# Small VectorE results in SBUF, shifts on GpSimd, an ELU scaled by e, and rows by two transfers, in a four-layer graph stack

## The chip, the cores and the metric

The kernel runs on one core of one Trainium2 chip. The metric is the device time of one execution in microseconds; the time of a kernel is the median of its runs. The profile tells five engines apart: PE (TensorE, the matmuls, with its weight loads as PEld), DVE (VectorE), ACT (ScalarE), POOL (GpSimd) and SP (SyncE, which here only issues DMAs).

## The reference

The input `x` has 32 batches of 512 nodes with 128 features; `adj` is one 512 x 512 matrix of zeros and ones for all batches. Four graph layers follow one another, each as `x = layernorm(x + layer(x, adj))`. The norm is over the 128 features, with no gain:

```
layer 0:  e = x a_i + (x a_j)^T            # 512 x 512 per batch
          e = leaky((e - mean(e)) / sqrt(var(e) + 1e-14) * adj + adj)
          out = sigmoid(softmax(e, axis=1) x)
layer 1:  h = x Wp + bp; scores = leaky(h a_src + (h a_dst)^T), filled where adj <= 0
          g = relu(layernorm(softmax(scores) * adj @ h))
          z = relu(layernorm(((1 + eps) g + adj @ g) W1 + b1))
          out = relu(z W2 + b2 + g)
layer 2:  A = softmax over the edges (a 512 x 512 constant)
          out = diag(A) x W[0] + (A - diag(A)) x W[1] + bias
layer 3:  h = x W; scores as in layer 1 with self loops
          out = elu(softmax(scores) @ h)
```

## The kernel before

**Tiles.** A batch is a tile of 128 partitions by 4 blocks by 128 features, `[P, NB, D]`, so one node of four stands on each partition. Score matrices are four tiles of 128 x 512, transposed (`e_r`, `nm_g`, `e_a`), and the sixteen 128 x 128 products of a layer go into PSUM (`p_o_r`, `p_o_g`, `p_o_a`). The suffixes name the layers: `_r` is layer 0, `_g` layer 1, `_t` layer 2, `_a` layer 3.

**Order.** No loop of the source sets the order in which instructions stand. A `Recorder` takes down every operation with what it reads and writes; `ORDER`, a compressed string, then says which of the operations that are ready is issued next, over all 32 batches and all engines. Each engine works through its list strictly in that order. So the batches overlap: layer 0 of one batch stands beside layer 3 of another. The costs in `cost` only choose buffers in `order()` and the few `warm` transposes that fill early PE gaps. Since every instruction is emitted by the recorder's `emit`, nearly all of the profile has one line, L434, and groups are told apart by the names of their tiles.

**PSUM.** Seven banks of 128 x 512 go round in a ring (`bank`). The eighth bank is `own`: half of it holds the constant `a_ij`, and in the rest `corner` (L516) gives small results a fixed place, four turns of each. Into it DVE writes the per-node maxima `top` of layers 1 and 3 (by the accumulator output of `any_g`, `any_a`, a `tensor_tensor_reduce`), mean and variance `mv` of the norms of layers 0 and 3 (by `bn_aggr`), the product `mr`, and in the statistics of layer 0 `mean_r`, a second copy of `dev_r`, and `sq_r`. In the profile all of these are called `own`.

**Norms.** `normalised` (L881, layers 0 and 3) takes `bn_stats` and `bn_aggr` on DVE, adds epsilon on DVE (`ve`), takes the power -1/2 on POOL (`rs`), multiplies mean by it on DVE (`mr`), makes the shift on DVE (`sh`), and lets ACT write `x = rs * y + sh` in four pieces. `scale_of` (L869, layers 1 and 2, whose mean is zero) does the epsilon and the power on POOL.

**Rows.** A column `[128, 4]` is needed as a row on all partitions in three places. `rows_of` (L922) does this with four PE transposes of a broadcast column into a bank; the row of layer 0, `p_s_r`, is made so. `rows_by_dma` (L928) does it for `top`: DVE transposes in blocks of 32 (`turned`), four DMAs on SP's queue write 4 x 32 elements each to a line in HBM (`linem_g`, `linem_a`), and one DMA reads the line back to all partitions (`m_g`, `m_a`).

**The ELU of layer 3** (L1193 to L1204): `po` is the unnormalised product in two banks and `rz` the reciprocal of its sums. ACT takes `ex = exp(po * rz)` in four pieces; POOL takes `min(ex / e, 1)` over 128 x 512; DVE takes the maximum of `po * rz` and that, in four pieces, in place in PSUM, and adds `x` in two pieces to get `y_a`. (The product carries an added 1, for which the division by e makes up.)

Of the kernel before, what the change touches and what calls it, by code (L numbers as in the profile page):

```python
# [14 lines left out]
AF = mybir.ActivationFunctionType  # L15
ALU = mybir.AluOpType

P = 128
# [17 lines left out]
TURNS = 4  # L36
# [9 lines left out]
c-k#m2bSxqmIaBNqd>uSh5O$BJ%*nDyn1t2JC!Zj2u|2Rs%>L}X}Ytq)2(lxw7qZ_-`l3PZ6lBRFaN&(d;O80^Up7C|M?Za_1`i2ckSf+`S<I1|Gt~1h  # L46
2C5}Ilu1D=Xu}sxadFMU$||Qeto?@@1M`>^P(sHyk9@`{hH6~{Y##kyk6w}+^>7!{`J5A^M3z_e8|7wpYQwq-{0R4ebfK_{D(ex^Y!mnd%pjJy<g4#d0
s!Rez`yQSN*O(q{^S~pYKb5*_Zi!-+!Jd?%(^KU;nCqzutH$<oioy`Sq2r?;knm=llKr;Xm(7yxw20`)hu_p7aXuar_zMGk&)3&(EK9#cz6ie*XFWH-1
LIFZ%a8{Mz~T{>?wx<@cYFKm8wi_CI(3rR~q3_Ryd9-TGG}<5hp^ul+9JC;!h+%ReRm_d9=OEH3M>VtzvX3Lyvmqo=Q_`5EU-GkWKW56K4~#<#EG^OfR
f&gVSq*PPkJ_B`>r?x<hSEH6=H>EgQ;nLp)KzG8mzJC+phoZ`Fp{BG^1q_3RP@&3HN;{Edd9bcb_7ks#q|9oEIm3<t?yT%yuD5;f{;tK=R5Yjt_cYnVy  # L50
*%U&(^XoXn(R*w$l@ddlCDr^+IfnXq$NFFzv5vHch{th+m`gtLSz^Q_M!)jw^$P3frRTG^BgY)$m1AqY_3~-8#d_45%5j#GV{J8*FvCcp{I}$@og?10m
(cq0(;ob&ttpjpwt1Y#`8AJz<QpGqPqp=a;MtEp@x@us>#VhY>UBRyDWhBkUn}u$?P{&e*iec`d9K`g=p*-z8HbBrC&|x~?)(07bB@{TKKq3sN5`aXI`
Yx0zcKX05t6mto{zQ1HEp%_84osGw%KBj+n$HD=TG_hndpnxnE9F4J@09+;f~85@vz<5j_Ev@&#<Gta`UAWmr_N@v8(p0eL{V?)7gMHTYr0h`0}yu`F>
~I;`K$Ji`4UHe##%@HQwp^xvub>pEF+H*X6Dsb6xiOy)N^8`}q6&{5sR#=6D(ZpMOm^x4G(Lvgv<*zh2KB{#>`wS?ltT*CuOoXj7xsHJ}TdGr5>_{OCN
gHM-mWWAqnBt^fRSe}13vPboj<`T8{<{rO2rGJBz<a2sj7j$`=eGmiB+eEj<z?%6+|@h-08&ZK|1SN`RzSMI@<$GP<R`!1*RJmWduzx{i@UiUGdyFKAP
+<DhBE4s#=ua)>&W=2_HPl+m|fY|wSRo@XAzf%%P#xwFGs*ZSx5~>Qe*U?NUF56^NGC+kh#u3HSQ4M_su!-xsioq<JDKA++wtcP=6!PKi=^CQM5w^m$c
9vz~YegZL!YAjPWo9_D(pfHivP3e)@X_KU7lsS`Et%(rCK7B@Q6fOCiB>R3RV?p&<|J@R@|KuqiTdOy%f&~gu|P_g^_F<=H{whP8%0aUxTgTf-y(Kwg|
L`+RMCbi*+e3{l3NfV?9zv=h@6wof+#CQ;RT1$Lg`I%NvtI->_i3{L=-y}fpZE<;TRaez<c)F?npwCs3FxLJVGl@q)<{2ahxs6sAP5`9X8m|fg#p-lLX
>}vKv`6`Uo1Rq{)bBbkq_*Wj@ln^L_V@icD$3@(J0AQq)U{w}OzWH1nI?#lC5`%Z-t3V;hq)bFm||%<tQVeG>d9HpcKCb7z=7UO8J&%JHH$#Wx%j3l@C
CMgdY={3tid@u2ubkw;GXj!)QR@n^$Sl=svo&8ua?2u9UTC62OFv-wRCFA|r#**9{qHDN}Wl0<OsaG(&i$GctjgEz+NzV96iWME~C-gu#V-7zYbf?a-B  # L60
JAS$oEr}6SGlXboY~S&2H(Ksk_L@HDI1b^2OS!VN?|jV}--HBU1hq&dQF+&z@ZIjjV3kCOY_dvHqV$!NMtG^cmcm&QA`%fiL(Yubky)!Y@0g(|S}(LQh
#I9@MP$IHEo!yzR7b3XkS67h(TZuCkyfy5xY{`lPNS+eOhHwHP+?)aJ(SQ^XvCHaO1Pn@G^$WYSXx#@qpy_N9oIz%ESwYVHs_pYPFbyR93><Yi9DKJ?@
H}V8KO7B3PF}A@x)!kt_<)Kf9<C2W(d&@Iw%s7=pG2)&_pO=?Tp4KmQsT{A)ChZ^@hl6ilK?$spDw1g!nn@JhJR0+AbIsqetwV#5`EGn2(@QlE8NAEz)
KUp%SrKtE6f}Sz>jlJDRhNQKAW*Pu>UTBJS4vnBw9D{4SMHQpmnFuy+QCRJ{Q%!k$d*(+w9~GS=Bivk9Yx>(UiqRr~~&oxu(5WmqJeLIST7=^#Q}Ob%N
iENV<GRTmdfmY#Ty-0~buXxwMW6a*fnTFh9ilSrVv2bZ1G)+P)fk}Ek2D;(-3sNknLhdn^8zI&2=y?|oEvJUWwHiyizXGp=GDJsrXWAbLU>a(a`G>j7j
an+H^-4MRJW{C;RgxFZwIM!;|jC;l~J@4@jELuQW^09e~Ab?w;jBsoD&bddZ6)e5R8ZTP{w1~eUTEOS&ZttF4Djf^YSCTzT*@{IjUgs%~I%O~NRit`qx
laYHBE2fuAuHakWF1}<BTbaj)+(E;TB#t_G)f(KGXZBl=_6<zyrwEuMI@r%Ys?~~DtS;saf|GTsA@=7A^Lfy9yL@)^12$-uELsi`Y1K)s5RG8Ggz-S%s
kYDOhkv5=1?PPsWNDY1l|pQby09Nx^}l~)~j7tydsLCU*W#b>$t9!d6ZJZhzSS22I}TI-E{7Dqd}yd$n8jZbPza>a=J00QqHu#n9d~`TM0ds0<CzZHB!
1zXW?F|Z^nYx@7%UVY9*DR?J}`XAV$B4x%KTauqF_Za~z#KZjwt>YDPitvZgXvuV=caz7Y~SM?t+jC(%D?l_(VB2vx_hx)xz>46LG2PHEF<>jd$VSL;L
%bRrh42$<5*;D<UEebgiM0-5`y0g*9kx?b1y6Timi%uh_YLm|)hT0}Cp#8YC)@9wY_?Q>c0AXYrY(6lApU;SJ$k7%%&eQ~Wu4`t_%;(bGyAb-#g{vLi<  # L70
+op|Ie^<XWV2i`nc-9Cy_p2{M@IAzU>~)B;$EEw(o+p1jr$q+m{XFM$y<VxjpiA!v9X|T&BKJ+=xbk_FaCzwZ(QwowlG9cH)9$-8R2J^BGzT$W78Zo28
<H351AScQl2hZk?(5Wty^e}LG<9ZV{(wr3m~;$a@#_1LAgkS|?$G$zfTV@c2OQDOS4zoIH%Eco-3-WrY)m^K)*%H^XIPd#fM;Qgo?e5ZB2*&>B;_RNuq
=_DilpTc#~3`Fz<-%ynka2d3r&^vbUIjVINF^<Xz6^SM2pE;htr`8@j$I|ms_ZlLr-JQ5P0bTw7F`RGON7vh$is>n#vb8@Lo7?^DLUT#A8EyT8Hv>60j
bmQ_|o_UcwLAq7#}HEes<kWDVRyLnRaZ(Nu@DNhn8-N+URMjRxz<@KT2*+*7wZC(M3BpaIo@Oz}YfqFOWY3%E!tfIss}Sz$rNLLY+ZinST=31N*mC+;-
&wP5~v33#3HM*_*ZSV*5LAj9zd*E~RZl>}*35wN1K*^;j43sXaLXpfHl2Gnkqv1&S?c8Bsz4hO7_8=iQHrXxBDkFhe%gAry5ld3S*dLxt*K!1@JnsK23
oaEFHvAo@9<z<Q!8aB^4wLA`mKuun|LA4nHG@Yjx{jcg4X=aW9MD!lsWgnIj?>yNnq2eyw+X={?J}m(sXNAKA1p;%rkI=v&>Cgc}==df2JJvdFGB6++^
A52h3s`z9sK9gC+|&acSn*}}*HKQ`K|dhH&)ndQD%uS9`WH5@;2r4K4#d>`r6up(Ovku;IST?a?#o7d;wYD0NIC+n@!_x-Z1Ms12iUL;XyAKWi%fIP5t
IrC2-|Wb);m4>))TZwx?fsPed(7zku9Cz#^B5@<j_Dq%tJMaJ`?;nsV5TO87dtLE?9|nmkI0yxi#>=ZtxLR)1o0M6iu5r0Er%CFWlH&4bj@LF>9DUG4K
$FIbh$(Itfr(T4e&GZGjhqz`wFiY=b1Zas|XEgoJvJLO_pGW>Vx~3m~0Zd{1Cg@a%{R^AJJ7ZNbEk09MY&b+iK<iwvMg(E~6%Z8VfKep*#i=p*oJg|=!
z%M*R&RCNIe2_q38K`Pp!B>~+OBL~=2J4QYLfek;ZFFc(=NvgEaAovuNuezmCd(EwY9w03TgZj?w>|?U@_e4bTN@dJ+&3m8~4&Pw#^IE?yMFIvSj)#_Y  # L80
6vH8>+0+6#7SM^{LFj;5(5#R~2nW$5>K&Smp^;&vQ{b8D-7D>9fhKW|@mjH2AqhH|=v4%(K-mGSl-GFKvxf438DG-CM&8h@iLapKBs{Pvz^HkdyptX}(
ra&n)KH;awmPW6t(!ozqzCo1C+J}guS1on*;)y04oyuri*0&Cr^Ce>3Hj|jd`O^?!p@@nax@5JLeK&<zspoC-=Kv~c71*O>yI4lV5O*5=&l^-p{HMz2g
pFbK*iY8V@vTydZ<`rG+?qLdjN8qXuE0#Caaf0ye|*W?dzlTef!%1A3_Fe0OC5VLq&xI>7kQ5I&9(M5eu^F4m39?4uuoD1Fr!+1NaaEV}MZMy3qfSD3#
h+Xhiwz%~~2Pg@c5bhAd5+-J;v9&XinkZeSSFVFH|{P8kIW6BJ1(I(iYLgLBELgZ<S;19G*2eZ~Mf+a@4Cs)o62=)eqcOsFCZ0iHotXiyYZGBu@CQH9b
@Z4c-@7ghP|Cjb((01>H*Y7q8mACUB`ecF7nqrdQgc)Hcur>{$0R|b)uI=6{Ac($bi>mo-Ugk})m488%ewQHK1z>N*4>AjS#LS`9*mdM>$vgA}7U}N7b
tOle$WOa(5!U(AjRL(L7R3@}kOa@ph4DcGIm&fQTfliPYXL(v#DgoW3fW)l|UW{AL1MLK=F&k7rywHY@@*)D@mVdCy!}U3@fh3#G@T7QzjAyk*+rROJ7
c|RnqWmlwR$*ES#ZB(XbiUY$7CRFgk<GvkJRrE>S`TI?<9zD0=-xm-CUBc`oWbeBgmbDn+Zfk7<LhL?j`n5LBG=54M3@{zM!7-7?iIS+?uRxOmCky0YM
jg+vKtn{Kx?{D0z@7Hx6ocfGPqdw2q_-pZc{Nk8f3O7K{MXS5>Uy2wGNn%6lox27bNfKOCCHGN_gv-+x147qD7^3c0z9qUU%D}s9~n|jP^vl)@g~LHs_
5qRy#%9MzMgCK%=XziAF``q$c5#gFSY_9RhfR?}Nn=f$H_Dz5+bLog`m!*@}WomIiPYgOEa0k$~b*5lHF<K#XvpP89Dzqt#_lZ_93p5Huo`NI^arsGcb
gOe@Nnb&wo{*waSklDrIvWi}aECdo4Rk(^0W4G^jGW0N;QhbX;My9G}P1`Y@W6jq$B#08OQ5!6HrxH6zb1Mi=d$R7F$wi)$R<ud1DFn<X20ce8_)*=X(  # L90
H3n(UCd3qjp{?+`Os}MQZ<sfLJBTbuDqbBk28DAN79mR0g#Iv*4QT9jk~7u@N<KPlSgq%T8K37YM;VA<ss_?vv1kt};V;BDAXViEjGMQApZ;<FfW^w^=
ly<O>h0h0=X^utf3D|w{Lk@zu;=GpK9J<i!6<<u^P$S4eh{a0s!^YLohYXF@tWYQp2nw#epaQ<e5y1RJg>s*;R9T%ss}npkzo7=Uq?CEB?&G7Je+_BGC
}MvU<K0}`k^pW0>{!(^DTFDYf`PX+R(EV-zi7e>@cu3=u-RwgtZ9H9<$el=`fE_C=i#;HM2@dyU~Gi-B&0gZ~}m#;EBQwKnVj?jNPzlP^1;ng2#QXcGo
# [138 lines left out]
def cost(engine, op, args, k):  # L232
# [10 lines left out]
    if engine == "dve":  # L243
# [4 lines left out]
        if op == "tensor_tensor_scan":  # L248
            return 60 + 2.08 * n, 85
# [12 lines left out]
    if engine == "pool":  # L262
# [992 lines left out]
```

## Time and profile before

| | |
|---|---|
| median of 3 runs | 1066.01 us (1064.12 to 1066.06) |
| profiled execution, its own time | 1064.63 us |
| span in the profile | 1062.9 us |
| mean granted TensorE clock | 0.976 |
| PE, DVE busy | 965.6 us, 954.7 us |
| ACT, POOL busy | 816.0 us, 770.0 us |
| DMA | 37.06 MB in 49606 packets |

Busy times are unions: where two instructions of an engine overlap in the record, the time counts once. Successive small DVE instructions do overlap, so what one of them costs is better read from the start of one to the start of the next. A matmul's end is modelled, so PE's busy time also holds some waiting.

### The profile page before, as it was taken

The page shows a single profiled execution, that of the slowest core. Times are in us where ns is not written, and L with a number is a line of the kernel's source. Part 1 is how long each engine was busy: PE and PEld are TensorE (multiplying, and loading weights), DVE is VectorE, ACT ScalarE, POOL GpSimd, SP SyncE. Part 2 cuts the span into 40 slices and gives each one's busy share as a digit, 9 for nine tenths or more (in the row PEclk, how much of TensorE's full clock was granted, in tenths as well). Part 3 has the DMA queues.
Part 4 walks back from the last instruction along what each step waited for, and adds up shares of the span by engine and source line. Part 5 has one row for each costly group of instructions (what it writes and reads, how often), then busy time and mean ns, then how long its engine had stood idle before and what let it go on. Part 6 is the DMA issues. An engine that isn't in the chain of part 4 may idle for free. (4 is left out here: it accounts for less than half of the span.)

```text
span 1062.9 us, 21689 instructions
## 1 busy us (share of the span) xinstructions
PE 965.6 (91%) x6583; PEld 794.6 (75%) x6583; DVE 954.7 (90%) x3635; ACT 816.0 (77%) x2399; POOL 770.0 (72%) x819
## 2 busy tenths in 40 slices
PE   7788999999999899899899998998989999999982
PEld 7778867677788678677768777787768778777772
DVE  7979997678989999999999989999989988978986
ACT  5899958667786878788788778978967996687573
POOL 7799755459784868669687686966776897358695
PEclk9989999999999999999999999999999999999996
DMA  7100000000011121001101111100110110010112
GB/s 196 29 21 22 22 10 24 9 21 17 15 41 41 31 61 41 21 12 46 55 21 42 38 52 43 31 21 22 31 40 21 32 31 11 22 50 21 32 42 59
DMA packets 49606, 37.06 MB, mean 35 GB/s; under 512 B 6353, under 2 KB 40785, under 8 KB 49489
## 3 DMA queue, kind: packets, MB, share of 16 engines
q1 hardware_dynamic: 49200, 35.15, 11.7%
q8 instruction: 52, 0.85, 0.3%
q14 instruction: 66, 0.53, 0.2%
q10 hardware_dynamic: 288, 0.52, 0.2%
HBM read 27.14 MB, written 8.52 MB: 34 GB/s over the span
## 5 line engine op out<-in xcount | busy, mean ns | idle before, releaser
L434 POOL TENSOR_TENSOR e_a<-e_a,m_a 128x512 f32<-128x512 f32 x128 | 161.4, 1279 | 18.7 <-DVE e_a L434 9.4
L434 POOL TENSOR_TENSOR e_r<-e_r,adj_t 128x512 f32<-128x512 f32 x128 | 160.6, 1278 | 14.1 <-ACT e_r L434 13.6
L434 PE MATMUL p_o_a<-h_a,e_a 128*128 128x129 f32 x1024 | 138.1, 282 | 10.5 <-ACT e_a L434 8.8
L434 PEld LDWEIGHTS p_o_a<-h_a,e_a 128*128 128x128 f32 x1024 | 128.4, 197 | 17.2 <-ACT e_a L434 10.3
L434 PE MATMUL p_o_r<-xs_r,e_r 128*128 128x128 f32 x1024 | 131.4, 282 | 7.3 <-DVE nm_g L434 2.7
L434 PE MATMUL p_o_g<-h_g,nm_g 128*128 128x129 f32 x1024 | 130.3, 276 | 4.5 <-DVE y_a L434 2.1
L434 PEld LDWEIGHTS p_o_r<-xs_r,e_r 128*128 128x128 f32 x1024 | 124.2, 197 | 13.1 <-POOL xs_r L434 3.8
L434 PEld LDWEIGHTS p_o_g<-h_g,nm_g 128*128 128x128 f32 x1024 | 122.1, 191 | 8.7 <-issue 3.3
L434 PE MATMUL p_y_t<-l_rest_t,x_g 128*128 128x512 f32 x256 | 122.4, 595 | 2.7 <-DVE hg_g L434 1.0
L434 PE MATMUL p_g_g<-a1t,hg_g 128*128 128x512 f32 x256 | 120.7, 594 | 0.2 <-DVE own L434 0.2
L434 ACT ACTIVATE e_a<-e_a,low_a 128x512 f32<-128x512 f32 x128 | 91.9, 735 | 26.3 <-POOL e_a L434 25.8
L434 ACT ACTIVATE p_e_g<-p_e_g,low_g 128x512 f32<-128x512 f32 x128 | 83.9, 665 | 29.7 <-DVE p_e_g L434 29.1
L434 ACT ACTIVATE e_r<-e_r,r_r 128x512 f32<-128x512 f32 x128 | 93.9, 742 | 7.4 <-POOL e_r L434 6.9
L434 DVE CUSTOM_DVE_ANT_0 any_g<-p_d_g,mask 128x512 f32<-128x512 f32 x128 | 88.2, 689 | 6.4 <-PE p_d_g L434 2.4
L434 DVE SCALAR_TENSOR_TENSOR p_e_g<-p_g_g,h_g,m_g 128x512 f32<-128x512 f32 x128 | 93.6, 749 | 0.2
L434 DVE CUSTOM_DVE_ANT_0 any_a<-p_d_a,mask 128x512 f32<-128x512 f32 x128 | 88.0, 687 | 5.9 <-PE p_d_a L434 1.8
L434 DVE SCALAR_TENSOR_TENSOR e_a<-p_g_a,h_a,mask_t 128x512 f32<-128x512 f32 x128 | 90.5, 740 | 1.8 <-PE p_g_a L434 1.8
L434 DVE SCALAR_TENSOR_TENSOR nm_g<-p_e_g,adj_t 128x512 f32<-128x512 f32 x128 | 86.6, 685 | 4.3 <-ACT p_e_g L434 4.1
L434 ACT ACTIVATE e_r<-p_s_r,tb_r 128x512 f32<-128x512 f32 x128 | 82.5, 707 | 3.1 <-PE p_s_r L434 2.7
L434 ACT ACTIVATE x_r<-y_r,sh_r,rs_r 128x128 f32<-128x128 f32 x128 | 54.1, 492 | 25.2 <-DVE sh_r L434 19.4
L434 POOL TENSOR_SCALAR ex_a<-ex_a 128x512 f32<-128x512 f32 x32 | 61.8, 1933 | 12.5 <-ACT ex_a L434 10.8
L434 PEld LDWEIGHTS p_g_g<-a1t,hg_g 128*128 128x128 f32 x256 | 44.1, 191 | 33.2 <-issue 31.4
(239 smaller groups left out, 2638.9 us busy)
## 6 DMA issues: line engine op xcount, KB each, us to landing
x_in<-in_x SPq DMA_DIRECT2D x32, 256.0 KB
m_g<-linem_g SPq DMA_DIRECT2D x32, 256.0 KB
m_a<-linem_a SPq DMA_DIRECT2D x32, 256.0 KB
out<-x_a SPq DMA_DIRECT2D x32, 256.0 KB
linem_g<-turnedm_g SPq DMA_DIRECT2D x128, 0.5 KB
linem_a<-turnedm_a SPq DMA_DIRECT2D x128, 0.5 KB
adj_n<-in_adj ACTq DMA_DIRECT2D x2, 256.0 KB
adj_n<-in_adj SPq DMA_DIRECT2D x2, 256.0 KB
```

The costliest lines, as they stand in the source:

```text
L434: f(*[real(a) for a in args], **{n: real(a) for n, a in k.items()})
```

## The change

Small DVE results go to SBUF tiles (`small`) instead of the bank `own`, which keeps only `a_ij`; the second copy of `dev_r` goes away. In `normalised`, epsilon, `mr` and `sh` are computed on POOL. `rows_by_dma` no longer transposes: one DMA writes the column `[128, 4]` straight to the line in HBM, element by element, and one reads it back. From batch 5 on (`ROWS_FROM`) layer 0's row is made in the same way instead of by PE. The ELU keeps e as a factor: ACT also writes `e * po * rz` into a new bank `q_a` in four pieces, DVE takes `max(min(ex, e), q)` and `x * e + q`, each over 128 x 512, and epsilon of the last norm is multiplied by e squared. `ORDER` is a new string; some figures in `cost` differ.

```diff
@@ constants
-TURNS = 4
+ROWS_FROM = 5
@@ ORDER: another string
@@ def scale_of / normalised
-    def normalised(dst, y, more, name, b, by_act=True):
-        mv = corner([P, NB, 2], "mv" + name, b)
-        statistics(y, mv)
-        ve = small([P, NB], "ve" + name)
-        R.dve.tensor_scalar(ve, mv[:, :, 1], LN_EPS, None, ALU.add)
-        r = power(ve, name)
-        mr = corner([P, NB], "mr" + name, b)
-        R.dve.tensor_tensor(mr, mv[:, :, 0], r, ALU.mult)
+    def normalised(dst, y, more, name, eps=LN_EPS, by_act=True):
+        r, mv = scale_of(y, name, eps)
+        mr = small([P, NB], "mr" + name)
+        R.pool.tensor_tensor(mr, mv[:, :, 0], r, ALU.mult)
         shift = small([P, NB], "sh" + name)
-        R.dve.tensor_scalar(shift, mr, -1.0, more, ALU.mult, ALU.add)
+        R.pool.tensor_scalar(shift, mr, -1.0, more, ALU.mult, ALU.add)
@@ def rows_by_dma
-        turned = buffer("turned" + name)[:, 0:32]
-        R.dve.transpose(
-            turned.rearrange("p (r c) -> p r c", c=NB), col.unsqueeze(1).to_broadcast([P, 32 // NB, NB])
-        )
         t = Tl(lines, "line" + name)
-        for c in range(NB):
...
-            R.sp.dma_start(part, turned[c:P:32, :])
+        line = V(t, (("__getitem__", (0,), {}), ("rearrange", ("(c p) -> p c",), {"p": P})), np.arange(N).reshape(NB, P).T.reshape(1, N))
+        R.sp.dma_start(line, col)
@@ def score_rows
-        top = corner([P, NB], "top" + name, b)
+        top = small([P, NB], "top" + name)
@@ def statistics0
-        mean = corner([P, 2, 2], "mean_r", bs[0] // GROUP)[:, 0:G, :]
+        mean = small([P, G, 2], "mean_r")
...
-            dev_p = corner([P, NB, 2], "dev_r", bs[0] + g)
-            for d in (dev, dev_p):
-                R.dve.tensor_tensor(
-                    d, n[:, :, 2 * g : 2 * g + 2], mean[:, g, :].unsqueeze(1).to_broadcast([P, NB, 2]), ALU.subtract
-                )
-            sq = corner([P, NB, 2], "sq_r", bs[0] + g)
-            R.dve.tensor_tensor_reduce(sq, dev_p, dev, 1.0, 0.0, ALU.mult, ALU.add, dev2[:, g : g + 1])
+            R.dve.tensor_tensor(
+                dev, n[:, :, 2 * g : 2 * g + 2], mean[:, g, :].unsqueeze(1).to_broadcast([P, NB, 2]), ALU.subtract
+            )
+            sq = small([P, NB, 2], "sq_r")
+            R.dve.tensor_tensor_reduce(sq, dev, dev, 1.0, 0.0, ALU.mult, ALU.add, dev2[:, g : g + 1])
@@ def layer0
-        p_s = rows_of(s, "s_r")
+        p_s = rows_of(s, "s_r") if b < ROWS_FROM else rows_by_dma(s, "s_r")
@@ def layer3
+        rze = small([P, NB], "rze_a")
+        R.pool.tensor_scalar(rze, rz, math.e, None, ALU.mult)
         ex = node_tile("ex_a")
+        q = blocks(bank("q_a"))
         for c in range(NB):
-            R.act.activation(ex[:, c, :], po[c // 2][:, c % 2, 0:D], AF.Exp, scale=rz[:, c : c + 1])
-        R.pool.tensor_scalar(ex, ex, math.exp(-1.0), 1.0, ALU.mult, ALU.min)
+            w = po[c // 2][:, c % 2, 0:D]
+            R.act.activation(ex[:, c, :], w, AF.Exp, scale=rz[:, c : c + 1])
+            R.act.activation(q[:, c, :], w, AF.Identity, scale=rze[:, c : c + 1])
+        R.dve.scalar_tensor_tensor(q, ex, math.e, q, ALU.min, ALU.max)
         y = node_tile("y_a")
-        for k, p in enumerate(po):
-            two = slice(2 * k, 2 * k + 2)
-            for c in range(2):
-                R.dve.scalar_tensor_tensor(
-                    p[:, c, 0:D], p[:, c, 0:D], rz[:, 2 * k + c : 2 * k + c + 1], ex[:, 2 * k + c, :], ALU.mult, ALU.max
-                )
-            R.dve.tensor_tensor(y[:, two, :], p[:, :, 0:D], xb[:, two, :], ALU.add)
+        R.dve.scalar_tensor_tensor(y, xb, math.e, q, ALU.mult, ALU.add)
         x4 = node_tile("x_a")
-        normalised(x4, y, 0.0, "_a", b, b < B - LATE)
+        normalised(x4, y, 0.0, "_a", LN_EPS * math.e**2, b < B - LATE)
```

## The prediction

> **What bounds it now.** First the page's busy times, then the engines by stretches, the groups by form, the waits, and last the timeline for the pace of small instructions.
>
> ```profile
> PE 965.6 (91%) x6583; PEld 794.6 (75%) x6583; DVE 954.7 (90%) x3635; ACT 816.0 (77%) x2399; POOL 770.0 (72%) x819
> ```
> ```profile
> core 0: us, PE busy (x) PEld busy (x) DVE busy (x) ACT busy (x) POOL busy (x), PEclk, DMA share, GB/s
> 0.00:50.00 50.00, 38.87 (x283) 35.62 (x284) 41.77 (x283) 31.95 (x70) 36.94 (x57) 0.96 0.48 119
> 50.00:100.00 50.00, 41.35 (x319) 39.17 (x318) 41.23 (x154) 46.24 (x119) 45.45 (x51) 0.91 0.07 23
> 300.00:400.00 100.00, 92.86 (x646) 76.32 (x646) 95.80 (x353) 76.90 (x235) 69.86 (x72) 1.00 0.13 38
> 500.00:600.00 100.00, 93.90 (x631) 74.67 (x630) 95.51 (x377) 79.25 (x241) 74.88 (x79) 1.00 0.14 41
> 1000.00:1063.00 63.00, 36.79 (x262) 34.02 (x260) 50.16 (x193) 32.35 (x77) 46.02 (x37) 0.81 0.18 51
> ```
>
> In the long middle DVE is fullest (the five stretches of 100 us from 300 to 800 average 94.7); PE looks close behind. PE's figure is modelled, so I also price it by pace: 32 `p_o_a` records take 3.65 us (0.114 each), successive `p_y_t` stand 0.43 apart, four `p_g_a` take 0.45. The page's counts give 4608 x 0.114 + 512 x 0.43 + 1152 transposes x 0.113 + 311 others x 0.114 = 911 us. So DVE bounds the middle, with PE some 40 us under it.
>
> ```profile
> L434 DVE CUSTOM_DVE_ANT_0 any_g<-p_d_g,mask 128x512 f32<-128x512 f32 x128 | 88.2, 689 | 6.4 <-PE p_d_g L434 2.4
> L434 DVE DVE_READ_ACCUMULATOR2_ANT own<- 128x1 f32 x256 | 36.3, 142 | 0.0
> L434 POOL TENSOR_SCALAR ex_a<-ex_a 128x512 f32<-128x512 f32 x32 | 61.8, 1933 | 12.5 <-ACT ex_a L434 10.8
> ```
> ```profile
> DVE p_o_a L434 <- POOL ex_a L434: 32.9, 28, 2.5
> ```
>
> The waits show one large stall of DVE, on POOL's pass of the ELU. The timeline shows what a small result in PSUM costs, by starts (start, duration):
>
> ```profile
> 620.67 0.69 DVE L434 CUSTOM_DVE_ANT_0 any_g<-p_d_g,mask 128x512 f32<-128x512 f32 x1
> 621.28 0.14 DVE L434 DVE_READ_ACCUMULATOR2_ANT own<- 128x1 f32 x1
> 621.46 0.69 DVE L434 CUSTOM_DVE_ANT_0 any_g<-p_d_g,mask 128x512 f32<-128x512 f32 x1
> ```
> ```profile
> 153.78 0.69 DVE L434 CUSTOM_DVE_ANT_0 q_t<-p_v_t,q_t 128x512 f32<-128x512 f32 x1
> 154.39 0.09 DVE L434 DVE_READ_ACCUMULATOR2_ANT l_mx<- 128x1 f32 x1
> 154.39 0.76 DVE L434 SCALAR_TENSOR_TENSOR p_e_g<-p_g_g,h_g,m_g 128x512 f32<-128x512 f32 x1
> ```
>
> With the accumulator in `own` the next instruction starts 0.79 us after the reduce; with it in SBUF (`l_mx`), 0.61 us.
>
> **DVE, part by part.** Maxima to SBUF: 256 x 0.18 = 46 us. `bn_aggr` of layers 0 and 3: four into `own` take 0.83 us, four `mv_t` 0.37, so 256 x 0.115 = 29. The norm's `ve`, `mr`, `sh` leave: by starts 0.07 + 0.20 + 0.08, 64 times, 22. `turned`: 64 x 0.13 = 9. The copy of `dev_r`: 32 x 0.20 = 6. ELU: four pieces in 1.13 and two in 0.75 become two instructions of the form of `y_g` (0.60 by starts): 32 x 0.68 = 22. Together 134, so DVE's 954.7 becomes 821.
>
> Against this stands a wait that before hardly has. `dev_r`, `sq_r` and both `bend` now have all inputs in SBUF: 128 instructions. The preparation shows what that can mean:
>
> ```profile
> 12.99 1.89 POOL L434 COPY mask<-mask 128x2048 f32<-128x2048 f32 x1
> ```
> ```profile
> 5.18 1.36 DVE L434 TENSOR_TENSOR_SCAN q_t<-edges 128x512 f32<-128x512 f32 x1
> 13.27 2.69 DVE L434 TENSOR_TENSOR_SCAN q_t<-edges 128x512 f32<-128x512 f32 x1
> ```
>
> A scan that needs 1.36 us took 2.69 when POOL's copy was running, ending 1.08 after the copy's end. Bounds for each of the 128: nothing (POOL idle), or one whole big POOL instruction, 1.28 us: 0 to 164 us. I take the random arrival: POOL is busy 72%, half an instruction remains, 0.72 x 0.64 = 0.46 us, 59 us in all. Less than nothing is excluded, since a port can't speed an instruction up. Queued behind each wait are all of DVE's next instructions; after `bend`, also the four PE transposes of `p_g`. The Trainium skill speaks against this part: its page SBUF — State Buffer, section "SBUF: two separate sides", says that DVE instructions with two SBUF inputs and GpSimd instructions lock each other out for a whole instruction. By it the small instructions wait as the scan did and 59 stays; were the scan a special case, the term would be 0.
>
> DVE then has 880 us of work, and 33 of its 108 us of idle time (the wait for `ex_a`) lose their cause. Late next in that place is ACT's last piece of `q`: before, four `exp` (1.26 us, at 0.31 by starts), POOL 1.93, DVE 1.88 = 5.1; after, eight ACT pieces 2.5 and DVE 1.2 = 3.7. It is not longer, so I put no stall back.
>
> **ACT** gains 128 pieces x 0.31 = 40, and 108 activations read `s_r` from SBUF (nearest rows 742 against 707 ns) = 4: 816 becomes 860.
>
> **POOL** loses 61.8 and gains per batch two norms of `ve` (0.230), `mr` (0.204, as `ve_go`), `sh` (0.230), and `rze` (0.230): 32 x 1.56 = 50. It falls to 758. The norm's chain stays about level: 0.23 + 1.03 + 0.20 + 0.23 on one queue, against the same power and three DVE steps with two changes of engine. Where a shift now queues behind a 1.28 us product, ACT's four `x` pieces and PE's next transposes wait for it; 64 norms bound this at 82 us. I take 0, because `x_r` before waits 19.4 us for `sh_r` already and ORDER interleaves other batches; the rest is in the range.
>
> **Rows.** PE loses 108 transposes x 0.113 = 12. SP issues 91 columns in place of 256 parts, so 0.5 us in place of 2.06 per row. A column is 512 elements of 4 bytes. No row shows such a write. All queue-1 packets took 11.7% of 16 engines' span over 49200, 40 ns each: 32 on each of 16 engines is 1.3 us; all on one engine, 20.7. A part's landing shows as 1.1 us from the end of its issue to the issue of `m_a`. So from issue to the read back: 0.5 + 1.1 + 1.3 = 2.9 against 3.2 now, with 1.6 to 22 as ends; I take 2.9, nearest to `a_col`, whose 256 elements were loaded before PE used them at 7.6 us with its issue at 1.7. The cover is the order: in the new one some 14 us of DVE work (4.3 at least) stands on average between the last maximum and the first use of `m_g`, by these paces, and 15 before. So the rows cost 0; if the column took 20 us, most of 32 x 9 us would show, and rows queued behind it on SP would be late too. The page DMA: Bandwidth & Descriptors, "Rules for kernel authors", advises against it as well: a strided last dimension becomes one descriptor per element. It gives no time for one, so nothing here rests on it.
>
> The new bank `q_a` and the bank that `p_s_r` no longer needs cancel: 0; a bank too few would show on PE, at most 32 x 1.2 us (ACT's added pieces).
>
> **The sum.** Three engines end close together: PE 911 - 12 = 899, DVE 880, ACT 860. PE now is the fullest. Outside the middle it idles 11.1 + 8.7 in the first two stretches and 26.2 in the last, 46, which I keep. In the middle DVE reached 94.7% as the fullest engine; with neighbours so near I take 93% for PE: 46 + 899 / 0.93 = 1013 us of span, with 1.7 us around it 1014.4. The profiled execution lies 1.4 under the median, so 1016. At 97% it is 976, at 90% 1048.
>
> **Rivals.** *PE binds as its busy rows say.* In 100 to 1000 these rows hold 849 us; less 12, at 94.7%, plus 163 is 1046, or 1049 on the median. For it: PE shows 99% in 150 to 250. Against: its own pace.
>
> *PSUM isn't what costs.* If the pace of 0.79 and the slow `bn_aggr` stay in SBUF, DVE keeps 75 us and stays at 955; only the wait for `ex_a` goes: 1033. The `l_mx` rows speak against it.
>
> *The port turns it slower.* On DVE at the four exposed instructions: POOL issues its products back to back, and if DVE loses the port to the next one as well, a wait is 1.5 us: 821 + 192 + 75 idle = 1088, 1091 on the median. It decides from a mean of (1063 - 75 - 821) / 128 = 1.30 us on, which is one whole POOL product each time. For it: runs of up to six `e_r` in 7.44 us. Against: the scan got the port at the end of one instruction.
>
> **Chances.** Forecast 0.60, PE binds 0.15, no relief from SBUF 0.05, port 0.12; 0.08 for what isn't listed, half of it slower. So faster 0.81, same 0.03, slower 0.16, where 0.2% (2.1 us) is about what a measurement of this kernel can tell from no change. The range runs from PE at 97%, 976, past both milder rivals to 1072, leaving out most of the port's case.
>
> **What would show it.** Right: `any_g` 0.61 apart, DVE's busy time near 880, no wait on `ex_a`, PE the fullest in 300 to 800. Each step wrong: `bend`, `dev_r` or `sq_r` starting a microsecond late beside a POOL product (port); DVE or POOL waiting for `m_g`, `m_a` or ACT for `s_r` (rows); POOL's `sh` behind products with ACT idle (norm); DVE idle before `p_q_a` (ELU). A time above 1049 means the port or the rows.

## The result and the profile after

The changed kernel takes 1176.44 us (median of 4 runs, 1174.98 to 1179.4) against 1065.27 us: a ratio of 1.105, 95% interval 1.102 to 1.107. The change makes the kernel 10% slower, and both the forecast of 1016 us and its range, 976 to 1072, miss it. The profiled execution took 1179.40 us, its span 1177.6 us, at a granted clock of 0.916 (before: 0.976).

First the page of the changed kernel: busy times, the clock in 40 slices, and the DMA packets.

```profile
PE 968.9 (82%) x6542; PEld 807.4 (69%) x6542; DVE 887.4 (75%) x3219; ACT 851.4 (72%) x2527; POOL 755.9 (64%) x1011
...
PEclk9959899799998899999898989979999998989977
...
DMA packets 99488, 44.15 MB, mean 37 GB/s; under 512 B 52784, under 2 KB 87216, under 8 KB 99376
...
q1 hardware_dynamic: 99088, 42.29, 21.1%
```

No engine is full any more, though DVE, ACT and POOL have almost the busy time that was forecast (880, 860, 758). Packets doubled: 91 columns of 512 elements are 46592 of them. The engines by stretches, columns as before:

```profile
50.00:100.00 50.00, 20.39 (x119) 15.87 (x118) 20.70 (x69) 13.83 (x28) 14.86 (x19) 0.69 0.30 42
...
300.00:400.00 100.00, 78.23 (x518) 63.49 (x517) 71.83 (x272) 69.61 (x216) 55.07 (x80) 0.91 0.17 31
...
500.00:600.00 100.00, 86.20 (x573) 73.33 (x573) 77.70 (x291) 76.64 (x225) 63.71 (x88) 0.90 0.21 37
```

In the middle every engine has idle time, DVE now about a quarter; between 50 and 100 us none is busy even half of the time, and the clock falls to 0.69. What they wait for, all engines and then SP's queue:

```profile
DVE p_e_g L429 <- DMA m_g<-linem_g: 107.5, 15, 28.0
...
POOL e_a L429 <- DMA m_a<-linem_a: 66.0, 8, 17.5
...
DVE xa_r L429 <- DMA x_in<-in_x: 25.6, 4, 15.1
```
```profile
SPq L429 <- DMA linem_a<-top_a: 267.6, 30, 11.3
SPq L429 <- DMA linem_g<-top_g: 239.7, 31, 10.8
SPq L429 <- DMA lines_r<-n_r: 105.3, 17, 10.9
```

DVE and POOL wait for the rows `m_g` and `m_a`, DVE even for the next batch's input. SP, which works through its list in order, waits 613 us for columns to land. In the kernel before, SP's waits for the same lines were these:

```profile
SPq L434 <- DMA linem_a<-turnedm_a: 22.4, 37, 1.8
SPq L434 <- DMA linem_g<-turnedm_g: 21.6, 40, 1.0
```

One column in SP's timeline (start, duration), and one row of the kernel before:

```profile
139.40 0.37 SPq L429 DMA_DIRECT2D linem_g<-top_g  x1
147.59 0.32 SPq L429 DMA_DIRECT2D m_g<-linem_g  x1
```
```profile
303.77 2.06 SPq L434 DMA_DIRECT2D linem_g<-turnedm_g  x4
306.94 0.33 SPq L434 DMA_DIRECT2D m_g<-linem_g  x1
```

From issue to read back it is 8.19 us in place of 3.17; over all rows `m_g` and `m_a` of the changed kernel it is 7.3 to 12.7. The forecast had put 2.9.

### The profile page after: what moved, and what is told of

It is laid out like the page before. It is cut to its first block, busy times and chain, and to the rows that moved or that the text cites. A ratio compares the mean times of both kernels' runs of the same rounds, so it can differ in the third digit from the quotient of the medians.

```text
span 1177.6 us, 21137 instructions
## 1 busy us (share of the span) xinstructions
PE 968.9 (82%) x6542; PEld 807.4 (69%) x6542; DVE 887.4 (75%) x3219; ACT 851.4 (72%) x2527; POOL 755.9 (64%) x1011
## 5 line engine op out<-in xcount | busy, mean ns | idle before, releaser
L429 PE MATMUL p_o_r<-xs_r,e_r 128*128 128x128 f32 x1024 | 162.1, 288 | 9.4 <-DVE dev_r L429 4.4
L429 PE MATMUL p_o_a<-h_a,e_a 128*128 128x129 f32 x1024 | 150.1, 280 | 22.6 <-ACT e_a L429 18.9
L429 PE MATMUL p_o_g<-h_g,nm_g 128*128 128x129 f32 x1024 | 159.0, 282 | 4.4 <-ACT p_q_a L429 4.1
L429 PEld LDWEIGHTS p_o_r<-xs_r,e_r 128*128 128x128 f32 x1024 | 144.7, 204 | 20.1 <-issue 17.6
L429 PEld LDWEIGHTS p_o_a<-h_a,e_a 128*128 128x128 f32 x1024 | 134.9, 196 | 33.8 <-ACT e_a L429 19.7
L429 PEld LDWEIGHTS p_o_g<-h_g,nm_g 128*128 128x128 f32 x1024 | 140.6, 198 | 12.6 <-issue 6.7
L429 PE MATMUL p_y_t<-l_rest_t,x_g 128*128 128x512 f32 x256 | 132.2, 633 | 17.4 <-DVE top_a L429 12.7
L429 DVE CUSTOM_DVE_ANT_0 any_g<-p_d_g,mask 128x512 f32<-128x512 f32 x128 | 83.1, 680 | 11.6 <-PE p_d_g L429 9.6
L429 PEld LDWEIGHTS p_y_t<-l_rest_t,x_g 128*128 128x128 f32 x256 | 45.6, 203 | 50.9 <-issue 34.4
L429 ACT ACTIVATE e_r<-s_r,tb_r 128x512 f32<-128x512 f32 x108 | 75.8, 728 | 0.0
L429 DVE CUSTOM_DVE_ANT_0 xa_r<-x_in,own 128x128 f32<-128x128 f32 x216 | 52.4, 277 | 25.7 <-DMA x_in<-in_x 25.6
```

What stands on the lines that cost most here:

```text
L429: f(*[real(a) for a in args], **{n: real(a) for n, a in k.items()})
```

## The experiments

The theory (A): the column written element by element lands late and holds up what is queued behind it. The rivals: the new order costs by itself (O), the port between DVE and POOL does (P), the added rows of layer 0 crowd SP's queue (C).

### The rows undone, the wait taken away, the column alone

**Rows in blocks.** The changed kernel with every row written as before, by a transpose and four parts.

```diff
-        R.sp.dma_start(line, col)
+        flip = flips.tile([P, 32], F32)
+        nc.vector.transpose(flip..., col broadcast to [P, 8, 4])
+        for c in range(NB):
+            nc.sync.dma_start(line part c, flip[c:P:32, :])
```

> The changed kernel with one part undone: every row (m_g, m_a and s_r) is written as before, by DVE's transpose and four parts of 32 runs of 128 bytes; all else is the changed kernel, its order too. Theory A (the column's landing): the waits for m_g (107 us on DVE) and m_a (66 us on POOL) fall below 20 us each, DVE's busy time grows by 91 transposes of 0.13, 12 us, and the time is 1010 to 1045 us, below the kernel before; the mean granted clock goes back above 0.95. Rival O (the new order or the lower clock by itself is what costs): 1130 us or more, with DVE waiting elsewhere. Rival P (the port between DVE and POOL): 1130 us or more, with the small DVE instructions late. Rival C (SP's queue is late because rows of layer 0 were added to it): about 1100 us or more, since four issues for each row load SP more than one.

Measured: 969.59 us (966.9 to 970.91), ratio to before 0.9105 (0.9084 to 0.9125), faster than A's range of 1010 to 1045. The row's way out turns 10% slower into 9% faster; the only other difference is 104 small buffers in place of 120, to make room for the transposed tiles. Page and waits of this kernel:

```profile
PE 930.8 (96%) x6542; PEld 778.9 (80%) x6542; DVE 893.2 (92%) x3310; ACT 846.2 (87%) x2527; POOL 755.7 (78%) x1011
...
PEclk9999999999999999999999999999999999999997
```
```profile
POOL e_a L429 <- DMA m_a<-linem_a: 4.3, 2, 2.4
DVE p_e_g L429 <- DMA m_g<-linem_g: 3.6, 2, 2.9
```
```profile
100.00:900.00 800.00, 789.67 (x5546) 657.58 (x5545) 747.89 (x2720) 726.18 (x2222) 618.23 (x825) 1.00 0.14 40
```

The waits for rows are gone, PE is the fullest engine (98.7% from 100 to 900 us) and the clock is at 0.988. O, P and C fall as causes of the loss. The same 6542 PE instructions are busy 930.8 us here and 968.9 in the changed kernel: of the 208 us between the two spans, 38 are longer busy time of PE, at a granted clock of 0.916 in place of 0.988, and 170 are PE idle. Why the clock is lower there no run took apart.

**Nobody waits for a column.** Columns are written, but the broadcast reads a row of `x`.

```diff
-        nc.sync.dma_start(pr, line broadcast)
+        nc.sync.dma_start(pr, x[0, 0:4, :] broadcast)
```

> The changed kernel, its columns still written, but the broadcast reads a row of the input x instead of the line, so that nothing waits for a column any more (the content of the rows m_g, m_a and s_r is left out of the computation). Theory A, as a pure latency of the column: the waits for m_g and m_a fall below 15 us, and the time is 995 to 1030 us. If the column's 512 elements instead keep the DMA rings busy for the 8 us, the broadcast issued behind it lands late all the same: m_g and m_a still wait, 40 us or more, and the time is 1050 to 1150 us. Rivals O and P (order, clock or port): 1130 us or more, without waits for m_g.

Measured: 1147.37 us (1145.02 to 1150.83), ratio 1.079 (1.076 to 1.082). Of the 207 us that columns cost, only 29 go when the broadcast no longer waits for the column. The waits show where the rest sits:

```profile
DVE p_e_g L429 <- DMA m_g<-in_x: 84.2, 13, 28.7
...
DVE xa_r L429 <- DMA x_in<-in_x: 22.9, 5, 8.1
```

A broadcast that depends on nothing that was computed still comes up to 28.7 us late. So the second branch of the expectation holds, and O and P, which expected no wait for `m_g`, fall: what is issued behind a column lands late. That goes for the row's own broadcast too, which for `m_g` and `m_a` SP mostly issues half a microsecond behind its column. So this run does not part a row's own lateness from that of the others behind it.

**The column in the kernel before.** Old order, maxima in SBUF, one column in place of transpose and parts.

```diff
-        R.dve.transpose(turned, ...); four R.sp.dma_start(part, turned...)
+        nc.sync.dma_start(line, col)
-        top = corner([P, NB], "top" + name, b)
+        top = small([P, NB], "top" + name)
```

> The kernel before with that part alone: the row's maxima in SBUF and one column DMA in place of the transpose and the four parts, in the order of before. DVE's busy time falls by about 46 (accumulators) and 9 (transposes) us. Theory A: each of the 64 rows lands about 5 us later than before, and waits for m_g and m_a of 60 us or more appear; the time is 1090 to 1200 us, slower than before. Rivals O and P: 1010 to 1040 us, faster than before, since the order and nearly all of the instructions that the port could delay are as they were.

Measured: 1163.98 us (1160.94 to 1170.01), ratio 1.095 (1.091 to 1.099), as A has it. 64 columns in the old order, with nothing else of the change beside them but the maxima's move, cost 100 us net. Its waits:

```profile
POOL e_a L434 <- DMA m_a<-linem_a: 105.0, 17, 16.2
...
DVE p_e_g L434 <- DMA m_g<-linem_g: 32.8, 11, 8.5
```

### Which columns

**m rows in blocks, layer 0's rows by column; and the other way round.**

```diff
+        if name != "s_r":     # first kernel; == "s_r" in the second
+            in blocks
```

> The changed kernel with the rows m_g and m_a written in blocks as before, and only layer 0's 27 rows s_r by columns. All rows in blocks gave 970 us, none 1176, a difference of 207. Theory A (each column holds up SP's queue and the DMA rings for about 8 us, whatever row it is): 27 of 91 columns remain, so 0.3 x 207 = 61 us, about 1030, between 1000 and 1060, and m_g and m_a wait again although they are written in blocks. Rival M (only the rows m_g and m_a cost, since they are wanted soon after they are written): 965 to 985 us. Rival C (the rows that the change added to the queue cost most): 1080 us or more.

> The other half: m_g and m_a by columns as in the changed kernel, layer 0's s_r in blocks. Theory A: 64 of 91 columns remain, 0.7 x 207 = 146 us, about 1115, between 1080 and 1150. Rival M (m_g and m_a are all of it): 1160 to 1180 us. Rival C: below 1060 us.

Measured: 992.39 us (991.64 to 994.67) with 27 columns, 1127.3 us (1118.93 to 1128.52) with 64, against 970 with none and 1176 with all 91. The second is near A's 1115; the first is below A's range, 7 us above M's, and M misses the second as well: a column does not cost the same wherever it stands. The 27 columns cost 23 us, and nearly all of that lies in one stretch, here in the kernel with 27 columns and then in the one with blocks alone:

```profile
50.00:100.00 50.00, 25.43 (x138) 19.12 (x136) 25.95 (x81) 18.73 (x41) 19.39 (x26) 0.73 0.22 43
```
```profile
50.00:100.00 50.00, 46.27 (x276) 34.94 (x275) 43.24 (x137) 37.76 (x98) 39.91 (x50) 0.97 0.09 28
```

PE is busy 21 us less there. SP's timeline of the kernel with 27 columns has the reason:

```profile
49.56 0.94 SPq L429 DMA_DIRECT2D lines_r<-n_r  x2
59.64 0.83 SPq L429 DMA_DIRECT2D s_r<-lines_r  x2
60.52 0.97 SPq L429 DMA_DIRECT2D lines_r<-n_r  x2
72.34 1.91 SPq L429 DMA_DIRECT2D s_r<-lines_r  x2
74.30 2.22 SPq L921 DMA_DIRECT2D linem_g<-turnedm_g  x4
```

From two columns to their reads it takes 10 to 12 us each time, and a row `m_g`, itself in blocks, stands behind them on SP; DVE waits 22.8 us for it at once. Later those columns hide. So what costs throughout is `m_g` and `m_a`. But beside them the 27 columns of layer 0 are not free: taking them away saves 49 us (1176.44 to 1127.3), although in the changed kernel ACT's 108 instructions that read the row `s_r` have no idle time before them (last figure):

```profile
L429 ACT ACTIVATE e_r<-s_r,tb_r 128x512 f32<-128x512 f32 x108 | 75.8, 728 | 0.0
```

So they cost through what stands behind them.

### What makes the column slow

Two kernels hold nothing but DMAs on SP's queue, each write followed by a small read back that waits for it.

```diff
+        nc.sync.dma_start(line view, data column or block)   # several shapes, 6 times each
+        nc.sync.dma_start(got, line[:, 0:4])
```

> The write of a row measured by itself, in several shapes, on SP's queue with nothing else running. The kernel leaves out the reference's whole computation (it copies one batch of x to every place of the output); only its DMAs are of interest. Each write is followed by a small read back that waits for it, so the distance from the write's issue to the read's issue is its landing. Theory A (the column's landing is what the change lost): a column of 512 elements of 4 bytes needs about 8 us from issue to read back, as SP's timeline of the changed kernel shows, and four parts in blocks about 3.2 us in all; if single elements are what costs, 128 elements need about 2.5 to 3.5 us and 1024 about 14 to 16 us, so 0.010 to 0.015 us for each element, and 128 runs of 16 bytes need no more than 128 elements do. Rival Q (the 8 us are the queue, busy with other work, and not the column): 512 elements alone land in 3 us or less, and 1024 hardly later. Rival S (the column is slow because of its 128 partitions): 128 elements need about as long as 512.

> Landings again, alone on SP's queue, the computation left out. So far: 128 single elements of 4 bytes out of 128 partitions needed 7.4 to 8.0 us, 1024 of them 9.2 to 11.6, and 128 runs of 16 bytes 1.4 to 2.9. Theory W (neighbouring 4-byte writes hinder each other, because they fall into the same few bytes of HBM): 128 elements of 4 bytes that lie 64 bytes apart in HBM land in 3 us or less, 16 neighbouring elements still take longer than that. Theory T (a 4-byte piece is slow wherever it goes): elements 64 bytes apart need 7 us as well, and so does a column to a row in SBUF; 32 and 16 elements need less. Theory S (it is the many source partitions): 128 elements read out of one partition land fast. Runs of 8 bytes lie between. Eight columns of 512 issued without a wait between them: if a column keeps the rings busy they need about 8 x 7 us, if its landing is only a latency about 10 to 15 us in all. A broadcast of 256 KB, which lands in about 3.1 us by itself, behind a column that it does not depend on: about 10 us if the rings are busy, about 3.5 if not.

Measured, from the start of the write's issue to the start of the read's issue:

| write | pieces | us |
|---|---|---|
| column of 128 / 256 / 512 / 1024 elements, HBM | 4 B, side by side | 7.3 to 8.3 / 8.0 to 11.2 / 8.7 to 10.6 / 9.2 to 11.6 |
| 32 / 16 elements, HBM | 4 B, side by side | 3.1 to 3.4 / 1.3 |
| 128 elements out of one partition, HBM | 4 B, side by side | 6.2 to 6.9 |
| 128 elements 16 B apart / 64 B apart, HBM | 4 B | 1.4 / 1.4 to 1.6 |
| 128 runs of 8 B / 16 B, HBM | 8 B / 16 B | 2.9 to 4.5 / 1.4 to 2.9 |
| four parts of 4 x 32 / one part, HBM | 128 B | 2.1 to 2.6 / 1.5 |
| column of 128 to a row in SBUF | 4 B | 1.9 to 2.7 |

Both Q and A's price for each element fall: 128 elements alone take 7 us, and eight times as many only 3 more. The first kernel by itself left S standing, which expected 128 elements to need about as long as 512; in the second S falls (one partition: 6.2 to 6.9), and so does T. W holds in part. From SP's timeline of the second kernel, a column of 128 and then 128 elements 16 bytes apart:

```profile
15.40 0.34 SPq L42 DMA_DIRECT2D column<-data  x1
23.68 0.23 SPq L40 DMA_DIRECT2D got_column<-column  x1
```
```profile
192.18 0.34 SPq L48 DMA_DIRECT2D apart16B<-data  x1
193.63 0.21 SPq L40 DMA_DIRECT2D got_apart16B<-apart16B  x1
```

The same 128 pieces of 4 bytes out of the same 128 partitions need 8.28 us side by side and 1.45 us with 12 bytes left free between them. It is neither the size nor the number of the pieces, but that many small ones lie next to each other in HBM. Nor is it the number of DMA engines: by the trace's completion events all 16 report in both cases, within 0.2 us of each other with the pieces apart, one after another from 3.3 to 8.3 us after the issue with the pieces side by side. W's wording went too far: at 16 bytes apart four still share 64 bytes, and 16 side by side are fast. What the memory does with them no run shows.

Eight columns of 512 without waits took 35 to 39 us to the last read, 4.4 to 4.8 us each (eight writes of 16-byte runs: 7.9 to 9.1 us, close to their issues). So eight columns neither follow each other freely nor wait for each other in full, between the two cases expected. In such a train the columns do hold the DMA engines: from 298.76 to 334.10 us, 4238 packets with 0.02 MB take 90.8% of the 16 engines' time. And a broadcast of 256 KB, first with nothing ahead of it, then behind a column that it does not read:

```profile
575.89 0.36 SPq L91 DMA_DIRECT2D behind_nothing<-in_x  x1
579.14 0.21 SPq L92 DMA_DIRECT2D back_nothing<-behind_nothing  x1
```
```profile
606.24 0.37 SPq L77 DMA_DIRECT2D l_column<-data  x1
607.10 0.33 SPq L91 DMA_DIRECT2D behind_column<-in_x  x1
616.05 0.24 SPq L92 DMA_DIRECT2D back_column<-behind_column  x1
```

3.25 us alone, 8.95 behind the column (8.6 to 11.1 in six). Yet the broadcast's packets are not late. The stretches of this trace (length, POOL busy, PEclk, busy share of the 16 DMA engines, GB/s):

```profile
607.10:610.40 3.30, 0.00 (x0) 1.00 0.47 80
610.40:616.05 5.65, 0.00 (x0) 1.00 0.00 0
```

The packets of both transfers are over by 610.40; then no packet runs for 5.65 us, and only after that does the read start that waits for the broadcast. By the completion events, each engine reports the broadcast 0.15 to 0.2 us after it reports the column. It is the same with a column of 128 alone: issued at 15.40, no packet after 16.50, read back at 23.68. So what is late here is not the packets but the report that the data has landed, the column's own and that of the transfer behind it. The Trainium skill, page DMA: Bandwidth & Descriptors, section "Queues, rings and completion order", says that the increment of the semaphore at the end of a DMA lands only after every earlier write of that engine; this pair agrees.

**Columns on ACT's queue.** The kernel in which nobody waits for a column, with the columns issued by ACT.

```diff
-        nc.sync.dma_start(line, col)
+        nc.scalar.dma_start(line, col)
```

> The kernel in which no row waits for a column (the broadcast reads a row of x, so the content of the rows is left out), 1147 us, with the columns issued on ACT's DMA queue in place of SP's. ACT issues 91 DMAs more, some 0.4 us each, 36 us of ACT's time, and may wait for DVE's maximum at some of them. Theory R (the columns hold up what is queued behind them on the same DMA queue): the waits for m_g, m_a and x_in go, and the time is 980 to 1040 us. Rival D (the columns hold up the 16 DMA engines for every queue): the waits stay, 1100 us or more.

Measured: 1035.34 us (1030.66 to 1041.96, and a fourth run of 1046.2), ratio 0.973 (0.967 to 0.980). That is 112 us less than with the columns on SP's queue and within R's range. The waits for `m_g` fall from 84.2 to 8.1 us, those for `x_in` from 22.9 to 6.5; one of 18.5 us for `s_r` stays. These are R's signs and not D's. But the run does not show that the other queue is the reason, because something else changed with it: SP no longer waits for the maximum before it issues the broadcast. One row, first on SP, then on ACT:

```profile
527.20 0.33 SPq L917 DMA_DIRECT2D m_g<-in_x  x1
```
```profile
534.14 0.37 ACTq L912 DMA_DIRECT2D linem_g<-top_g  x1
```

Of the 91 broadcasts 81 are now issued ahead of their column, about 7 us in the middle; with the columns on SP's queue all were issued behind it. So neither R nor D is settled: how much of the 112 us is the queue and how much the earlier issue stays open. A run that holds the broadcasts back until the column is issued would tell. The same page of the skill, section "Issuing engines are not separate DMA queues", says that issuing from several engines saves only the time of issue; for the same reason this run can't decide that. The other 66 us above the blocks were not taken apart, but SP's transfers are still slowed: its queue's packets take 32.1% of the 16 engines' span, against 15.4% with rows in blocks.

### What the parts are worth when rows are in blocks

**Maxima back in PSUM.** The kernel with blocks, `top` in the bank `own` again.

```diff
-        top = small([P, NB], "top" + name)
+        top = own[:, a free corner]
```

> The kernel with all rows in blocks (970 us), with the maxima of layers 1 and 3 put back into the PSUM bank, as before the change. By the prediction's pace each of the 256 maxima then takes DVE 0.18 us more, 46 us. Theory A (DVE's saving was real and with its 893 us of busy time beside PE's 931 it is near the bound): the maxima stand 0.79 us apart again, and DVE's 46 us show in part, 985 to 1010 us. Rival E (PE binds alone, and DVE's saving bought nothing): 967 to 975 us. Rival F (the small results in PSUM cost DVE nothing but the longer record of the accumulator's read): the maxima stay 0.61 us apart, 967 to 975 us.

Measured: 992.26 us (990.13 to 995.77), 23 us more. The saving on the maxima is real, and half of the 46 us in the sum: DVE's busy time went from 893.2 to 910.4, and `bend_g` and `bend_a`, which then read one input from PSUM, lost 5 us of waits, so the 256 maxima took some 23 us of busy time more, 0.09 each. They stand 0.79 us apart again (the median). F and E fall; A holds in its lower half.

**Rows by runs of 16 bytes.**

```diff
-        transpose and four parts
+        nc.sync.dma_start(line.rearrange("(p c) -> p c", c=4), top)   # m_g, m_a
+        # p_e_g and e_a read the row with a step of 16 bytes
```

> The kernel with all rows in blocks (970 us), but m_g and m_a are written by one DMA of 128 runs of 16 bytes (each partition's four maxima side by side in the line), without DVE's transpose; the two instructions that read the row read it with a step of 16 bytes. By itself such a write landed in 1.4 to 2.9 us, a column of 128 single elements in 7.5 us. Theory G (it is the 4-byte piece that is slow, not the number of pieces or of partitions): SP's waits for these lines stay under 3 us each, DVE loses 64 x 0.13 = 8 us, and the time is 955 to 975 us. Rival H (any write of 128 pieces holds up the busy rings): 1030 us or more. Rival I (the strided read is what costs): e_a or p_e_g take over 0.1 us longer each, 128 of each, and the time is 980 to 1000 us.

Measured: 1017.05 us (1015.55 to 1018.28), ratio 0.956 (0.954 to 0.958). Neither of the two instructions waits for its row here, and SP's waits for these lines are 1.5 us on average (3.8 at most, above G's 3); H falls. But the time is above G's range and, by 17 us, above I's of 980 to 1000. The groups show I's cause:

```profile
L1082 DVE SCALAR_TENSOR_TENSOR p_e_g<-p_g_g,h_g,m_g 128x512 f32<-128x512 f32 x128 | 144.7, 1148 | 2.5 <-ACT x_g L429 1.2
...
L1183 POOL TENSOR_TENSOR e_a<-e_a,m_a 128x512 f32<-128x512 f32 x128 | 195.0, 1549 | 12.1 <-DVE e_a L429 11.8
```

With blocks these take 746 and 1276 ns. The step of 16 bytes adds 0.40 us on DVE and 0.27 on POOL, 128 times each: 51 and 35 us of busy time, well over I's 0.1 us each.

**Rows by way of SBUF.** 4-byte pieces into a row of SBUF, from there in one piece to HBM.

```diff
-        R.sp.dma_start(line, col)
+        for c in range(NB):
+            nc.sync.dma_start(row[:, block c], col[:, c : c + 1])   # row: one partition of SBUF
+        nc.sync.dma_start(line, row)
```

> The changed kernel, its rows still written as columns of 512 pieces of 4 bytes and without DVE's transposes, but into a row of SBUF (four DMAs of 128 pieces, one for each block), from there in one piece to the line in HBM, and then broadcast. Alone, 128 such pieces landed in SBUF in 1.9 to 2.0 us and the line in 1.1 after that, where the same pieces side by side in HBM took 7.3 to 8.3. Theory W (only 4-byte pieces that lie side by side in HBM are slow): the row needs about 2.1 us of issues, 1.5 of landing and 1.1 for the line, SP's waits for these DMAs stay under 2.5 us each, m_g and m_a wait less than 20 us in all, and the time is 955 to 985 us; 91 transposes of 0.13 us less than the kernel with rows in blocks (970 us), and a longer way for the row. Rival N (512 pieces of 4 bytes hold up a busy queue wherever they go): 1050 us or more. Rival Q (the longer way and 273 more issues delay SP's queue): waits for m_g or x_in of 30 us or more, 985 to 1020 us.

Measured: 987.13 us (986.53 to 987.52), ratio 0.927 (0.926 to 0.929), 2 us above W's range. SP's waits:

```profile
SPq L927 <- DMA rows<-top_a: 40.3, 42, 2.3
...
SPq L927 <- DMA rows<-top_g: 37.9, 42, 2.2
```

None is over 2.3 us for `m_g` and `m_a`; the lines from SBUF to HBM take SP 2.0 us at most for these rows and 3.1 for layer 0's. The same 512 pieces of 4 bytes, bound for SBUF, do not hold up SP, and N falls. The time, 17.5 us over the blocks, lies in Q's range, but the waits are less than Q's 30 us, and nearly all of it arises at the start, behind layer 0's rows: PE is busy 30.3 us from 50 to 100 against 46.3, with one wait of 17.6 us for `m_g`. So the four parts in blocks stay the best of the ways tried, and the changed kernel with them, at 970 us, beats both kernels.

## Why the prediction was wrong

**Rows: the step that failed.** The sum put a column at 2.9 us from issue to read back and concluded that "the rows cost 0". Measured are 7.3 to 12.7 us for `m_g` and `m_a` in the kernel and 8.7 to 10.6 alone, inside the ends of 1.6 to 22, and the 91 columns cost 207 us together. The choice of 2.9 was made with a time for each packet, 40 ns, a mean over packets that were nearly all larger, shared evenly by 16 engines. But the time is hardly in the packets: those of a column of 128 are over 1.1 us after its issue, and for 7.2 us none runs. No row of the trace of before showed such a write, and the row that it was called nearest to (`a_col`) bounds only an arrival, at 5.9 us.

What the sum lacked is what stands behind a column. It counted the cover for the row itself (14 us of DVE work), and for SP only the shorter issue. But SP waited 613 us for columns before it could issue the next DMA of its list, and where it did not wait (1147 us) the broadcasts behind the columns were late all the same; the 27 columns of layer 0, whose rows nobody is seen to wait for, are worth 49 us. How much of the 207 us is a row's own lateness no run parts, so the cover of 14 us is neither shown nor refuted. The sentence on rows behind it was there, but for a column of 20 us. "A time above 1049 means the port or the rows" pointed to the right place.

**Without the column the forecast was too high.** With rows in blocks the kernel takes 970 us where the sum gives 1016, although it has 12 us more of transposes. PE did become the fullest engine, as forecast. The two terms around it were too large: idle at both ends 28 us (9.9 up to 100, 18.1 after 900) in place of 46, and PE's 899 us of paced work fill the remaining 941 to 95.5%, not 93%. The rival that read PE's busy time (1049) was farther off; that busy time itself fell to 930.8, where the rival left it at 953.

**DVE: right by two errors.** 880 us were forecast, 887.4 measured. But the saving was 74 us, not 134, and the port 7, not 59; the two misses nearly cancel, which is luck. The largest part of the 134, the maxima, was made from starts (0.79 against 0.61), and part of such a distance can be idle time, which a busy time does not hold: the maxima put back cost 23 us of busy time, not 46. The other 37 us were not taken apart. The pace itself was read rightly; the median is 0.61 us in the changed kernel, and here two reduces follow at 0.62:

```profile
306.68 0.69 DVE L429 CUSTOM_DVE_ANT_0 any_a<-p_d_a,mask 128x512 f32<-128x512 f32 x1
307.30 0.09 DVE L429 DVE_READ_ACCUMULATOR2_ANT top_a<- 128x1 f32 x1
307.30 0.69 DVE L429 CUSTOM_DVE_ANT_0 any_a<-p_d_a,mask 128x512 f32<-128x512 f32 x1
```

**Port: a few waits, not the size.** Minimum, median and maximum of `bend_g` before and after, in ns:

```profile
L434 DVE SCALAR_TENSOR_TENSOR bend_g<-own,h_g x32: 118/151/163, 59.2 to 920.4; 128x4 f32<-128x4 f32 x32
```
```profile
L429 DVE SCALAR_TENSOR_TENSOR bend_g<-top_g,h_g x32: 127/153/1108, 52.8 to 1038.0; 128x4 f32<-128x4 f32 x32
```

A few wait about 1 us, half take no longer than before. The means of the four groups rose by 33 to 85 ns, 7 us for 128. The Trainium skill's rule (SBUF — State Buffer, "SBUF: two separate sides") made every such instruction wait out a running GpSimd instruction; these rows do not show that. In the changed kernel 38 of the 128 started while a POOL instruction had more than 0.2 us to run, and only ten of these took over 0.4 us. Why so few wait is open.

**Right.** ACT 851 us (forecast 860), POOL 756 (758), the wait on `ex_a` gone, and the norm's chain at no cost: ACT's `x_r` waits 0.9 us for POOL's `sh_r`, where it had waited 19.4 for DVE's. The place of the ELU shows 18.5 us of DVE's wait on `p_q_a` in the changed kernel, but 3.3 with rows in blocks: it was part of the standstills.

## What to carry to other kernels

A DMA has two prices: the time until its own data lands, which the order of work can cover, and the time by which it delays what stands behind it, on the engine that waits for it and on its queue; add the second over all transfers before calling one hidden. Packet times do not hold either price: here they were over long before the landing was reported. A shape of transfer that the trace does not hold should be measured alone first: six issues with a read back would have shown 8 us. And a saving worked out from starts belongs in a sum of starts, not in one of busy times.

## What the runs showed of the hardware that was not expected

- Pieces of 4 bytes are not slow as such: 128 of them land in HBM in 1.4 us if they lie 16 bytes apart, in 7.3 to 8.3 us side by side, and in SBUF in 1.9 to 2.7 us.
- A broadcast behind a column on the same queue takes 8.6 to 11.1 us instead of 3.1 to 3.4, though its packets are over in about 3.3 (none runs from 610.40 to 616.05): what is late is the report that it has landed.
- A second input read with a step of 16 bytes costs DVE 1148 ns instead of 746 and POOL 1549 instead of 1276. The Trainium skill (SBUF — State Buffer, "Door 1: The DMA port swizzle") says that reads that cross to a new 16-byte line each time pay a penalty; it gives none, these rows do.
- PE's granted clock was lower where PE idled more: 0.988, 0.976, 0.935 and 0.916 at PE shares of 96, 91, 85 and 82%, with the rows in blocks, before, with columns that nobody waits for, and in the changed kernel. The order is not strict: with runs of 16 bytes it was 0.991 at 93%.
